# A two-layer relational graph convolution: each ring buffer of ten gathered row tiles is filled and read in the opposite direction on every other pass

## The chip, the cores and the metric

The kernel runs on one core of a Trainium2 chip. The metric is the device time of one execution in microseconds (us), as the median of three runs; lower is better.

## The reference

There are N = 50000 nodes with D = 128 numbers each, 850000 edges sorted by their destination, 16 relations and 8 basis matrices. Two layers of a relational graph convolution are followed by a residual sum and a layer norm. Everything is in 32-bit floats.

```python
def _rgcn_layer(h, src, dst, rel, basis, w_comp, loop_w, bias):
    W = jnp.einsum('rb,bio->rio', w_comp, basis)            # 16 x 128 x 128
    seg = dst * 16 + rel
    agg = jax.ops.segment_sum(h[src], seg, num_segments=50000 * 16)
    agg = agg.reshape(50000, 16, -1)
    msg = jnp.einsum('nri,rio->no', agg, W)
    return jax.nn.relu(msg + h @ loop_w + bias)

h = _rgcn_layer(x, src, dst, rel, basis1, w_comp1, loop_w1, bias1)
h = _rgcn_layer(h, src, dst, rel, basis2, w_comp2, loop_w2, bias2)
return _layernorm(x + h)
```

The heavy part is `h[src]`: for every edge, a row of 128 floats (512 B) has to be fetched from a place in memory that an index gives.

## The kernel before, in words

**Tiles and chunks.** 128 edges make a tile. K = 10 tiles make a chunk, and a layer has C = 625 chunks (800000 edges; each node's edge to itself is treated apart, without a gather). The layers are the rounds n = 0 and n = 1 of one loop: layer 0 reads its rows from `x`, layer 1 from `H1`, the DRAM tensor that layer 0 wrote. In all there are 1250 chunks and 12500 tiles.

**Gathers.** One gather fetches the 128 rows of one tile by an indirect DMA of the Pool engine (`gather`, L198). Every gather of the program has this line, because the line is the helper's. It writes slot k of a row buffer. There are GATHERS = 6 row buffers of ten slots each, used in turn as a ring: chunk c of layer n has buffer `(n * C + c) % GATHERS`.

```python
for to in range(0 if c == 0 else c + FETCH, min(C, c + FETCH + 1)):
    for k in range(ks(to)):
        gather(rows[(n * C + to) % GATHERS][:, k, :], of, src[:, to * K + k : to * K + k + 1])
```

`ks(to)` is the number of tiles of a chunk (ten). FETCH = 2 fixes only the place of the gathers in the program's text. The engines run apart from each other, each through its own instructions in order, so Pool runs ahead until it would overwrite a slot that TensorE has not read yet.

**What a chunk does.** For each tile, TensorE multiplies the gathered rows (as the stationary operand) with `hot`, a 128 x 96 matrix that VectorE makes (`hot_of`, L782 and L789) and that says which of the tile's up to 12 destinations an edge belongs to, weighted for the 8 bases (L837, tile `pa`). Five tiles (PER = 5, half a chunk) share one PSUM bank; after them ScalarE copies the bank to `aT` (L844). So a chunk has two halves, each with five gathers' rows, five multiplications and one copy. Each fp32 multiplication shows as two TensorE records in the profile.

**What lies between.** Between the two halves of chunk c, `slots` multiplies `aT` of chunk c - 1 with the eight bases, all accumulating in `ps` (L689), and ScalarE copies the result (L693). Ahead of the first half, `nodes_of` adds up the slots of chunk c - 2 by node (L703, L707, tile `pn`; VectorE's sum L709; ScalarE's `kept`, L712) and stores the nodes' result. The nodes' own parts (`from_itself`, 391 tiles of 128 nodes per layer) are spread over the chunks, at most chunks one and at some none: a transpose (L205), its copy `hT` (L207), the product with the bases `hb` (L667), which VectorE weighs (L670) and reduces (L681), and a store (L682). In layer 0 a preparation of later rows (`coming`) runs between the chunks too; Pool takes part in it with twenty scatters.

**Who sets the order.** TensorE's and Pool's instructions run in the order in which the program writes them (a manual schedule for these two engines). The waits between the engines are put in by the framework from what reads and writes which tile: an instruction that overwrites a slot waits for the semaphore of the engine that read it, unless its engine has already waited for that point or a later one. Ahead of an instruction that needs a second wait stands a semaphore instruction of its own.

Of the kernel before, what the change touches and what calls it, by code (L numbers as in the profile page):

```python
# [64 lines left out]
PER = 5  # L65
Q = AT // 2
GATHERS = 6
# [9 lines left out]
def tile_rgcn_resnorm(  # L77
# [20 lines left out]
    C = -(-M // (K * P))  # L98
# [98 lines left out]
    def gather(to, of, idx):  # L197
        nc.gpsimd.indirect_dma_start(  # L198
            out=to, out_offset=None, in_=of, in_offset=bass.IndirectOffsetOnAxis(ap=idx, axis=0)
        )  # L200
# [382 lines left out]
    def chunked():  # L583
        with (
# [5 lines left out]
            def at(c):  # L590
                return nc.values_load(
                    base_i[0:1, c : c + 1],
                    engines=[mybir.EngineType.SP],
                    min_val=0,
                    max_val=N - P,
                    skip_runtime_bounds_check_because="bases are clamped to N - P, and no node is below 0",
                )

            def weights(c, n):

                m = min(AT, 2 * (C - c)) * NR
                rel = hp.tile([P, LIVE], U8, name="rel")
                nc.sync.dma_start(
                    rel[:m],
                    bass.AP(
                        tensor=REL.tensor, offset=REL.offset + 2 * c * LIVE, ap=[[LIVE, m // NR], [0, NR], [1, LIVE]]
                    ),
                )
                is_rel = hp.tile([P, LIVE], F32, name="is_rel")
                nc.vector.tensor_scalar(is_rel[:m], rel[:m], its_rel[:m], None, op0=OP.is_equal)  # L610
                yield
                pm = ps_m.tile([P, AT * PER * NB], F32, name="pm")
                of = pm.rearrange("e (t j) -> e t j", t=AT)
                for j in range(PER):
                    nc.tensor.matmul(  # L615
                        of[:, :, j * NB : (j + 1) * NB],
                        is_rel[:m, j * P : (j + 1) * P],
                        EACH[n][:m],
                        start=True,
                        stop=True,  # L620
                    )
                yield pm.rearrange("e (t b) -> e t b", b=NB)
# [104 lines left out]
            def asked(c):  # L727

                return min(NT, -(-(c + 1) * NT // C) + AHEAD)
# [40 lines left out]
            for n, of in enumerate((x, H1)):  # L770

                kept, summed_up, multiplied, lws = None, None, None, []
                base, ks = [at(0), None, None], lambda c: min(K, -(-M // P) - c * K)
                own_parts = []

                def own_nodes(c):

                    return range(asked(c - 1) if c > 1 else 0, asked(c) if c else 0)

                def hot_of(c, pm):  # L780
                    own = hp.tile([P, K, WN], F32, name="own")
                    nc.vector.tensor_tensor(  # L782
                        own[:, : ks(c)],
                        grid[:, None, :WN].to_broadcast([P, ks(c), WN]),
                        key[:, c * K : c * K + ks(c), None].to_broadcast([P, ks(c), WN]),
                        op=OP.is_equal,
                    )
                    hot = hp.tile([P, K, NB, WN], F32, name="hot")
                    nc.vector.tensor_tensor(  # L789
                        hot[:, : ks(c)],  # L790
                        pm[:, c % Q * K : c % Q * K + ks(c), :, None].to_broadcast([P, ks(c), NB, WN]),
                        own[:, : ks(c), None, :].to_broadcast([P, ks(c), NB, WN]),
                        op=OP.mult,
                    )
                    return hot

                def loaded(n0):

                    ls = sb.tile([P, D], F32, name="ls_of")
                    nc.sync.dma_start(ls, L[n][ds(n0, P), :])  # L800
                    xw = None
                    if n:
                        xw = sb.tile([P, D], F32, name="xw")
                        nc.sync.dma_start(xw, x[ds(n0, P), :])
                    return ls, xw

                weigh = weights(0, n)
                next(weigh)
                for c in range(C):
                    now[0] = c  # L810
                    if n == 0 and c:

                        next(coming, None)
                        while ready[0] + 1 < len(ROWS) and 2 * min(C, c + FETCH + 4) > ROWS[ready[0] + 1]:
                            next(coming)
                    if c:
                        base = [at(c)] + base[:2]
                    for to in range(0 if c == 0 else c + FETCH, min(C, c + FETCH + 1)):
                        for k in range(ks(to)):
                            gather(rows[(n * C + to) % GATHERS][:, k, :], of, src[:, to * K + k : to * K + k + 1])  # L820
                    g = rows[(n * C + c) % GATHERS]
                    if c == 0:
                        if n == 0:
                            done(first_runs)
                        pm = next(weigh)
                        hot = hot_of(c, pm)
                    if c > 1:
                        kept = nodes_of(kept, c - 2, ks(c - 2), summed_up, base[2], *others, n)
                        others = loaded(base[1])
                    parts = own_parts[0] if own_parts else iter(())  # L830
                    next(parts, None)
                    aT = hp.tile([P, NB, S], F32, name="aT")
                    for k in range(0, ks(c), PER):
                        m = min(PER, ks(c) - k)
                        pa = ps_a.tile([P, BANK], F32, name="pa")
                        for i in range(m):
                            nc.tensor.matmul(  # L837
                                pa[:, i * NB * WN : (i + 1) * NB * WN],
                                g[:, k + i, :],
                                hot[:, k + i].rearrange("e b w -> e (b w)"),  # L840
                                start=True,
                                stop=True,
                            )
                        nc.scalar.copy(  # L844
                            aT[:, :, k * WN : (k + m) * WN].rearrange("d b (i w) -> d i b w", w=WN),
                            pa[:, : m * NB * WN].rearrange("d (i b w) -> d i b w", i=m, w=WN),
                        )
                        if k == 0:
                            next(parts, None)
                            if c:  # L850
                                summed_up = slots(c - 1, ks(c - 1), multiplied, n)
                            next(parts, None)
                    multiplied = aT
                    for parts in own_parts:
                        done(parts)
                    if c == 1:
                        others = loaded(base[1])
                    if c + 1 < C:
                        if (c + 1) % Q == 0:
                            pm = next(weigh)  # L860
                        hot = hot_of(c + 1, pm)
                        if c + 2 < C and (c + 2) % Q == 0:
                            weigh = weights(c + 2, n)
                            next(weigh)
                        own_parts = []
                        for i in own_nodes(c + 1):
                            own_parts.append(from_itself(i, of, n, lws))
                            if len(own_parts) == 1:
                                next(own_parts[0])
                    if n == 0 and c == 3:  # L870
                        beginning.close()
                    if n == 0 and c == C - 1:
                        done(coming)
                        count_up(pr)
                last = loaded(base[0])
                kept = nodes_of(kept, C - 2, ks(C - 2), summed_up, base[1], *others, n)
                summed_up = slots(C - 1, ks(C - 1), multiplied, n)
                nodes_of(kept, C - 1, ks(C - 1), summed_up, base[0], *last, n)
# [189 lines left out]
```

## Time and profile before

| what | value |
|---|---|
| median of three runs | 18938.22 us (18929.84 to 18953.83) |
| the profiled execution | 18936.72 us |
| its span, from first to last instruction | 18934.8 us |
| granted TensorE clock, mean | 0.72 of full speed |
| TensorE matmuls (PE) | 10703.0 us, 57% of the span, 59198 records |
| TensorE weight loads (PEld, overlap PE) | 9174.1 us, 48% |
| VectorE (DVE) | 6595.5 us, 35% |
| ScalarE (ACT) | 2775.4 us, 15% |
| Pool (POOL) | 11864.7 us, 63%, 12533 instructions |
| DMA queue of the gathers (q0) | 403552 packets, 826.82 MB, 16.8% of 16 engines' time |
| all transfers | 1227.02 MB, mean 65 GB/s |

How to read the lines of this profile. A group of instructions is named by its line (L198 is line 198 of the kernel), engine, operation, and tiles: `g<-H,src` writes a row buffer `g` from `H` by the indices in `src`. Behind `x` is the count, behind the first bar the busy time in us and the mean of one in ns, behind the second bar the idle time of the engine just ahead of such instructions and what ended it. A row of the waits has the waiting engine, tile and line, then what let it go, then the sum of these waits in us, their number, and the longest of them. "issue" is time in which the engine waited for nothing that the profile shows. "remote" means that a semaphore let the instruction go, but no instruction or transfer that the profile shows ended near that moment. A row of the timeline has the start in us from the span's start, the duration, the engine, the line, what was done, and in brackets the idle time ahead of it with its releaser.

### The profile page before, as it was taken

What the parts mean: (1) busy time and instruction counts of PE and PEld (TensorE: products, weight loads), DVE (VectorE), ACT (ScalarE), POOL (GpSimd) and SP (SyncE); (2) the same over time, 40 slices, a digit from 0 to 9 for tenths busy, and PEclk for the clock granted to TensorE, in tenths of its full rate; (3) what the DMA queues carried; (4) which work ended last, traced back from release to release, by engine and by line L of the source; (5) the groups of instructions that cost most, each with busy time, mean ns of one, the idle gap of its engine ahead of it and who ended that gap; (6) DMA issues with size and microseconds to landing.
All of it is one profiled execution on the core that took longest, in us unless ns stands there. A gap on an engine that the chain in (4) does not pass through costs nothing.

```text
span 18934.8 us, 187693 instructions
## 1 busy us (share of the span) xinstructions
PE 10703.0 (57%) x59198; PEld 9174.1 (48%) x59198; DVE 6595.5 (35%) x14269; ACT 2775.4 (15%) x7815; POOL 11864.7 (63%) x12533
## 2 busy tenths in 40 slices
PE   4555555555555555555555555555555555555555
PEld 3444445444544445445445555445454444444445
DVE  4333334333333332333223333333333333333333
ACT  1111111111111111111111111111111111111111
POOL 5666666665666666666656666666666666666665
PEclk7777777676777776777767777777777777777777
DMA  2222222222222222222222222222222222222222
GB/s 80 69 69 65 68 66 66 66 66 63 62 62 61 61 61 61 61 61 61 61 55 66 67 66 67 66 66 67 65 66 66 66 66 66 65 66 66 66 65 62
DMA packets 1164943, 1227.02 MB, mean 65 GB/s; under 512 B 283055, under 2 KB 952401, under 8 KB 1163937
## 3 DMA queue, kind: packets, MB, share of 16 engines
q0 software_dynamic: 403552, 826.82, 16.8%
q1 hardware_dynamic: 757169, 386.65, 7.1%
q8 instruction: 472, 7.73, 0.2%
q14 instruction: 534, 4.37, 0.1%
q10 hardware_dynamic: 3216, 1.45, 0.0%
HBM read 1059.55 MB, written 154.23 MB: 64 GB/s over the span
## 4 chain that ended last, share of the span: by engine, by line
another core or an unknown queue 22%; PE 17%; issue 7%; DVE 5%; ACT 2%; DMA 0%; POOL 0%; SPq 0%; ACTq 0%; DVEq 0%; POOLq 0%
PE pa L837 6%; PE ps L689 4%; PE hb L667 4%; DVE ls L681 1%; DVE by L670 1%; DVE hot L789 1%; PE pn L703 1%; ACT aT L844 1%; PE pn L707 1%; PE po L678 0%; PE po L205 0%; DVE by L679 0%; ACT slots L693 0%; ACT sd L574 0%
## 5 line engine op out<-in xcount | busy, mean ns | idle before, releaser
L198 POOL DMA_INDIRECT g<-H,src x6250 | 5910.6, 946 | 3393.7 <-issue 1422.2
L198 POOL DMA_INDIRECT g<-in_x_dram,src x6250 | 5927.4, 948 | 3338.4 <-issue 1411.5
L837 PE MATMUL pa<-hot,g 128*128 128x96 f32 x25000 | 4125.3, 326 | 1898.8 <-DVE hot L789 1388.2
L837 PEld LDWEIGHTS pa<-hot,g 128*128 128x128 f32 x25000 | 4014.2, 243 | 2402.1 <-DVE hot L789 1434.6
L689 PEld LDWEIGHTS ps<-basis,aT 128*120 128x120 f32 x20000 | 3222.4, 240 | 927.1 <-issue 849.3
L667 PE MATMUL hb<-basis,hT 128*128 128x512 f32 x3128 | 2273.3, 818 | 2107.1 <-ACT hT L207 915.7
L689 PE MATMUL ps<-basis,aT 128*120 128x128 f32 x20000 | 3211.3, 329 | 224.3 <-issue 150.5
L670 DVE TENSOR_TENSOR by<-hb,lw 128x512 f32<-128x512 f32 x1564 | 1080.1, 691 | 6152.1 <-remote 2557.6
L789 DVE TENSOR_TENSOR hot<-pm,own 128x960 f32<-128x960 f32 x1250 | 1432.6, 1153 | 4113.1 <-remote 3585.2
L844 ACT COPY aT<-pa 128x480 f32<-128x480 f32 x2500 | 1395.2, 558 | 6619.3 <-remote 3577.7
L703 PE MATMUL pn<-slots,own 120*128 120x128 f32 x2500 | 708.5, 373 | 2448.5 <-ACT slots L693 1502.1
L703 PEld LDWEIGHTS pn<-slots,own 120*128 120x128 f32 x2500 | 470.3, 235 | 2593.2 <-ACT slots L693 1583.3
L667 PEld LDWEIGHTS hb<-basis,hT 128*128 128x128 f32 x3128 | 638.1, 253 | 2191.4 <-ACT hT L207 943.1
L681 DVE TENSOR_REDUCE ls<-by 128x128 f32<-128x1152 f32 (+1 forms) x782 | 1656.9, 2119 | 12.1
L693 ACT COPY slots<-ps 120x128 f32<-120x128 f32 x1250 | 332.4, 266 | 5771.4 <-remote 3733.1
L205 PE MATMUL po<-ident,h_own 128*128 128x128 f32 (+1 forms) x782 | 295.8, 378 | 1151.9 <-issue 399.5
L205 PEld LDWEIGHTS po<-ident,h_own 128*128 128x128 f32 (+1 forms) x782 | 138.1, 177 | 1219.9 <-issue 415.1
L707 PE MATMUL pn<-kept,shift 128*128 128x128 f32 x2496 | 604.8, 332 | 12.1 <-DVE shift L706 6.3
L615 PE MATMUL pm<-each,is_rel 128*128 128x64 f32 x3140 | 438.6, 281 | 114.4 <-issue 110.4
L707 PEld LDWEIGHTS pn<-kept,shift 128*128 128x128 f32 x2496 | 493.7, 245 | 14.2 <-DVE shift L706 7.7
L712 ACT COPY kept<-pn 128x128 f32<-128x128 f32 x1248 | 336.1, 269 | 1079.7 <-DVE a L709 603.5
L709 DVE TENSOR_TENSOR a<-pn,ls_of 128x128 f32<-128x128 f32 x1250 | 355.1, 284 | 386.6 <-remote 133.1
(148 smaller groups left out, 5082.0 us busy)
## 6 DMA issues: line engine op xcount, KB each, us to landing
g<-in_x_dram,src POOLq DMA_INDIRECT x6250
g<-H,src POOLq DMA_INDIRECT x6250
ls_of<-L SPq DMA_DIRECT2D x1250, 64.0 KB
L<-ls SPq DMA_DIRECT2D x780, 64.0 KB
H<-h SPq DMA_DIRECT2D x625, 64.0 KB
xw<-in_x_dram SPq DMA_DIRECT2D x625, 64.0 KB
out_dram<-o SPq DMA_DIRECT2D x625, 64.0 KB
h_own<-in_x_dram SPq DMA_DIRECT2D x390, 64.0 KB
```

What stands on the lines that cost most here:

```text
L198: nc.gpsimd.indirect_dma_start(out=to, out_offset=None, in_=of, in_offset=bass.IndirectOffsetOnAxis(ap=idx, axis=0))
L205: nc.tensor.transpose(tp[:, :m], h, ident[:m, :m])
L615: nc.tensor.matmul(of[:, :, j * NB : (j + 1) * NB], is_rel[:m, j * P : (j + 1) * P], EACH[n][:m], start=True, stop=True,)
L667: nc.tensor.matmul(hb[:m], hT, BASIS[n][:, b : b + few, :].rearrange("p b d -> p (b d)"), start=True, stop=True)
L670: nc.vector.tensor_tensor(by[:m, b : b + few, :], hb[:m].rearrange("p (b d) -> p b d", d=D), lw[:m, b : b + few, None].to_broadcast([m, fe ...
L681: nc.vector.tensor_reduce(ls[:m], by[:m].rearrange("p b d -> p d b"), AX.X, OP.add)
L689: nc.tensor.matmul(ps[: k * WN], aT[:, b, : k * WN], BASIS[n][:, b, :], start=b == 0, stop=b == NB - 1)
L703: nc.tensor.matmul(pn, own[: k * WN], st[: k * WN], start=True, stop=not c)
L707: nc.tensor.matmul(pn, shift, kept, start=False, stop=True)
L789: nc.vector.tensor_tensor(hot[:, : ks(c)], pm[:, c % Q * K : c % Q * K + ks(c), :, None].to_broadcast([P, ks(c), NB, WN]), own[:, : ks(c), ...
L837: nc.tensor.matmul(pa[:, i * NB * WN : (i + 1) * NB * WN], g[:, k + i, :], hot[:, k + i].rearrange("e b w -> e (b w)"), start=True, stop=True,
L844: nc.scalar.copy(aT[:, :, k * WN : (k + m) * WN].rearrange("d b (i w) -> d i b w", w=WN), pa[:, : m * NB * WN].rearrange("d (i b w) -> d i ...
```

## The change

Chunks are counted over both layers, `n * C + c`, and the count divided by six (the number of buffers) gives the pass over the ring. On an even pass nothing differs from before. On an odd pass the ten gathers of a chunk fill the slots from 9 down to 0, and the ten multiplications read them in that order: the second half first, and within each half the last tile first. The `slots` step and the own-node steps stay between the half that is read first and the one that is read second. No instruction of another kind is added, and none of the gathers, multiplications or copies is removed. `base`, `hot_of`, the ring of buffers, FETCH and the order of the chunks are untouched.

```diff
+                def in_turn(c, k, of=None):
+
+                    of = of or range(k)
+                    return list(of)[:: 1 - 2 * ((n * C + c) // GATHERS % 2)]
+
...
                     for to in range(0 if c == 0 else c + FETCH, min(C, c + FETCH + 1)):
-                        for k in range(ks(to)):
+                        for k in in_turn(to, ks(to)):
                             gather(rows[(n * C + to) % GATHERS][:, k, :], of, src[:, to * K + k : to * K + k + 1])
...
-                    for k in range(0, ks(c), PER):
+                    halves = list(range(0, ks(c), PER))
+                    for k in in_turn(c, len(halves), halves):
                         m = min(PER, ks(c) - k)
                         pa = ps_a.tile([P, BANK], F32, name="pa")
-                        for i in range(m):
+                        for i in in_turn(c, m):
                             nc.tensor.matmul(
...
-                        if k == 0:
+                        if len(halves) == 1 or k == halves[in_turn(c, len(halves))[0]]:
                             next(parts, None)
                             if c:
                                 summed_up = slots(c - 1, ks(c - 1), multiplied, n)
```

A buffer is thus refilled in the reverse of the order in which it was last read: the slot that was read last is written first.

## The prediction

> **What bounds the kernel now.** I read the page from the top: busy time, groups, the chain, then the waits, then stretches of the timeline. No engine is full:
>
> ```profile
> PE 10703.0 (57%) x59198; PEld 9174.1 (48%) x59198; DVE 6595.5 (35%) x14269; ACT 2775.4 (15%) x7815; POOL 11864.7 (63%) x12533
> another core or an unknown queue 22%; PE 17%; issue 7%; DVE 5%; ACT 2%; DMA 0%; POOL 0%; SPq 0%; ACTq 0%; DVEq 0%; POOLq 0%
> L198 POOL DMA_INDIRECT g<-H,src x6250 | 5910.6, 946 | 3393.7 <-issue 1422.2
> L198 POOL DMA_INDIRECT g<-in_x_dram,src x6250 | 5927.4, 948 | 3338.4 <-issue 1411.5
> ```
>
> A gather is 0.95 us busy and 0.30 us of "issue", a pitch of 1.25 us, and POOL does nothing else of weight: 12500 x 1.25 = 15625 us of the 18934.8. The rest is stops. The largest share of the chain belongs to no engine, so I ask the waits who waits there:
>
> ```profile
> ACT slots L693 <- remote: 3733.1, 551, 49.8
> DVE hot L789 <- remote: 3585.2, 428, 24.9
> ACT aT L844 <- remote: 3577.7, 570, 35.9
> POOL g L198 <- PE pa L837: 1621.8, 1277, 33.9
> POOL g L198 <- remote: 1586.1, 1153, 8.9
> ```
>
> Every "remote" row of size waits on TensorE's own semaphore, at a time when no matmul ended by the profile in the 1.5 us before. So a matmul's completion is seen late. A table of stretches shows when (after the stretch: PE, PEld, DVE, ACT, POOL busy with counts, granted clock, DMA share, GB/s):
>
> ```profile
> 9593.00:9618.00 25.00, 24.39 (x202) 24.04 (x200) 10.02 (x26) 8.54 (x24) 0.00 (x0) 0.93 0.11 31
> 9645.00:9715.00 70.00, 10.89 (x36) 8.07 (x36) 0.69 (x1) 0.83 (x2) 52.94 (x57) 0.52 0.20 53
> ```
>
> In the first, POOL is silent (all gathers of layer 0 are issued): PE is full and a chunk takes 4.42 us. In the second POOL gathers without a pause into buffers that are long free, and everything else stands still. The timeline inside it:
>
> ```profile
> 9648.38 3.35 PE L689 MATMUL ps<-basis,aT 128*120 128x128 f32 x16
> 9662.53 0.56 ACT L844 COPY aT<-pa 128x480 f32<-128x480 f32 x1 [20.14 <-remote]
> 9668.08 0.69 DVE L670 TENSOR_TENSOR by<-hb,lw 128x512 f32<-128x512 f32 x1 [25.33 <-remote]
> 9712.87 0.27 ACT L693 COPY slots<-ps 120x128 f32<-120x128 f32 x1 [49.79 <-remote]
> ```
>
> The `ps` matmuls end at 9651.7 by the profile; ScalarE is let go for them at 9712.87. So back-to-back gathers hold back what the other engines may see of each other. In the steady part this makes a cycle: POOL gathers until the ring of six buffers is full, stops, completions come through, POOL goes on.
>
> ```profile
> 9050.44 0.94 POOL L198 DMA_INDIRECT g<-in_x_dram,src  x1 [0.30 <-issue]
> 9053.60 0.94 POOL L198 DMA_INDIRECT g<-in_x_dram,src  x1 [2.22 <-remote]
> 9054.84 0.94 POOL L198 DMA_INDIRECT g<-in_x_dram,src  x1 [0.30 <-issue]
> ```
>
> Counted over all gathers of the trace (a stop: next start over 1.5 us later; gather n is slot n mod 10 of its chunk): 1473 stops, 3190 us. 447 stand before slot 0 (1538 us, median 2.8), 734 before slot 5 (1359 us, median 2.0), 292 elsewhere. Updates of TensorE's semaphore recorded per us: 1.2 in a run's first two gathers, 0.3 from the fourth on, 0.1 from the twentieth; 0.4 in the first half us of a stop, 1.6 in the next, 7.2 between 1.5 and 2.0 us. So each stop first costs some 1.5 us of nothing, and each restart gives about 3 us of free progress. The mean chunk, from chunk 60 to 1200, takes 15.04 us; 1250 x 15.04 = 18800 leaves 137 us for start and end of the profiled execution's 18936.7, which is 1.5 us under the median of the three runs, 18938.2. So: time = 137 + 1250 x cycle.
>
> **The change, part by part.** *Order of reading and of filling.* The same 25000 matmul records, 2500 copies and 12500 gathers, in another order; within a chunk a matmul still reads the slot that was gathered at the same place of the order. Nothing by itself. POOL's two scatters of the preparation (20 in all) keep their places between chunks.
>
> *Waits that go.* Now each gather waits for TensorE's reading of its own slot six chunks ago, and has one semaphore instruction before it (12506 on POOL). After it, the first gather of a chunk writes the slot that was read last; when it may go, so may the other nine, which should lose their wait on TensorE and most of their semaphore instructions. Price of these: 4316 gathers with none between them and the gather before start after 0.305 us (median), 3057 with two also after 0.305. They hide behind the gather ahead. If that cover were gone, the recorded 0.017 us x some 11000 = 190 us. I take zero.
>
> *The wait that is added.* The first gather now waits for the tenth matmul and not for the first; queued behind it are nine gathers. Those who need their rows are the matmuls of six chunks later: from a gather's end to its matmul the trace has 82.7 us (median, first slot; 78.4 the last; 5% under 71). The delay is at most from first half to last: 8.6 us between the two `aT` copies of a chunk. The rows stay early.
>
> *The stops.* What remains is the rhythm: POOL no longer starts when half a chunk is free, and no longer stops at slot 5; it gathers ten without a pause, then stops until the last matmul of the next chunk is seen. The trace has that very situation, shifted by five slots: a run that starts at slot 5 (second half just seen) and goes on for ten. From 687 such starts to the copy of the next chunk's second half:
> - 367 runs (53%) go exactly ten gathers: 15.0 us. Kept.
> - 117 (17%) go 11 to 14 and then take 18.1, having begun a second burst on single slots. After the change they stop at ten: I take 15.0.
> - 112 (16%) go 15 or more: the half was seen in time. They become runs of twenty. Now, after fifteen, POOL stops 3.5 us for the first half of the next chunk, and the second half is seen 7.3 us later. Twenty gathers take 25 us; the stop behind them lies between 5.0 (then the pair takes 30, as now) and 10.8 (3.5 + 7.3). Nearer the low end, as TensorE has had six more us: 6.5, the pair 31.5.
> - 91 (13%) stop before ten, since TensorE is late. That stop now comes after the tenth, after more starving: between 15.0 and 12.5 + 6.1 = 18.6; I take 16.0.
>
> Per 99 starts: 70 x 15.0 + 16 x 31.5 + 13 x 16.0 = 1762 us for 115 chunks, 15.32 us. 137 + 1250 x 15.32 = **19290 us**, 1.9% slower. With the low ends 15.0 (18890), with the high ones (doubles 35.8, late 18.6) 16.2 (20390).
>
> Two rules weighed. The row: PE's clock is 0.52 in the starved stretch and 0.93 in the free one. The Trainium skill (TensorE: Matmul & The Clock Gate, HAM oscillation) says that pauses over some 3.4 us put TensorE back to half clock; longer unbroken bursts make more such pauses, which speaks against the change; if every matmul ran at half clock, PE's 10703 us at 0.72 would be 15400, 12.3 us a chunk. And where the rows show completions held back by gathers, the skill (DMA: Bandwidth & Descriptors, Anatomy of one DMA) calls a DMA's semaphore write almost free on trn2; by that nothing would be held back and POOL alone would set 12.5 us a chunk before and after, which the 70 us stretch contradicts.
>
> **Rivals.** *One stop a chunk pays (faster).* There are 1.18 stops a chunk now, 2.16 us each. If every cycle locks into the exact run of ten with the 2.0 us stop that follows it in the trace (372 cases, quartiles 1.98 to 2.09), the cycle is 14.5: 18290; with some late halves 14.9: 18760. For it: 74% of the runs before a chunk that has an own-node part go exactly ten. Against: before chunks without one only a third do. It decides if stops of over 4 us stay under one in ten.
>
> *Relief (faster).* If POOL's waits on TensorE's semaphore are what holds it back, they go, and POOL is bound at 12.5 us: about 15800. Against: the first 60 gathers (44 to 121 us) wait on no matmul, and TensorE's updates come 5.6 us apart there too.
>
> *Nothing happens.* The framework keeps ten per chunk, or the cycle stays by chance at 15.0: 18940.
>
> **How the numbers follow.** Slower as worked out: 0.58 (own range 18980 to 20390). One stop pays: 0.30. Relief: 0.04. Nothing: 0.08, which is all within 0.2%, about what a measurement of this kernel can tell from no change. Faster is 0.30 + 0.04 = 0.34. The range leaves out relief, the lowest part of the locked case, and the slow tail: 18450 to 20200.
>
> **What would show it.** Right: runs of gathers only in multiples of ten, all stops before the first gather of a chunk, gather pitch still 1.25 us, "remote" still the largest waits, some stops of 5 us and more behind runs of twenty. Wrong: stops nearly all at 2.0 us (locked), or almost no stops and full TensorE clock (relief). A pitch under 1.25 us would make the semaphore instructions a cost after all.

## The result: 3.8% slower, and the profile after

The changed kernel takes 19651.8 us (median of four runs, 19629.3 to 19667.7) where the kernel before takes 18934.0: a ratio of 1.0378, 95% interval 1.0360 to 1.0396. The forecast said slower, by 1.9% (19290); the time lies inside the range, but the loss is 718 us where 352 were forecast, twice as much. The profiled execution took 19629.3 us, its span is 19627.5, the granted clock 0.716 (before 0.720).

The page of the changed kernel: busy time, the chain, and the two groups of gathers.

```profile
PE 10992.7 (56%) x59198; PEld 9425.0 (48%) x59198; DVE 6594.1 (34%) x14269; ACT 2779.3 (14%) x7815; POOL 11894.5 (61%) x12533
another core or an unknown queue 21%; PE 17%; issue 8%; DVE 5%; ACT 1%; POOL 0%; DMA 0%; DVEq 0%; ACTq 0%; SPq 0%; POOLq 0%
L198 POOL DMA_INDIRECT g<-H,src x6250 | 5933.2, 949 | 3793.8 <-issue 1732.5
L198 POOL DMA_INDIRECT g<-in_x_dram,src x6250 | 5934.5, 950 | 3633.5 <-issue 1739.9
```

The number of gathers is the same and their price nearly so (946 and 948 ns before, 949 and 950 now). The idle time ahead of gathers grew from 6732.1 to 7427.3 us, by 695.2: as much as the two spans differ, 692.7. The "issue" part of it hardly matters: between gathers that follow each other the mean pitch is 1.2526 us before and 1.2521 after. So the time went into stops. The waits of the changed kernel (lines have moved by up to six: L850 is the `aT` copy, L794 `hot`, L843 `pa`):

```profile
ACT aT L850 <- remote: 5097.1, 725, 28.9
DVE by L670 <- remote: 4226.5, 347, 49.7
DVE hot L794 <- remote: 3514.0, 480, 53.7
POOL g L198 <- remote: 1390.9, 591, 11.1
POOL g L198 <- PE pa L843: 1374.5, 211, 27.6
POOL g L198 <- PE po L678: 988.8, 121, 16.4
```

"remote", the completions that are seen late, still lead. Pool's waits for TensorE are fewer and longer: 923 in these three rows, 4.1 us in the mean, where the two rows of before have 2430 of 1.3 us. In the third row it is a product of an own-node part (`po`) that ends the wait. Counted over all gathers: 1050 stops and 3889 us, before 1473 and 3196. 956 of the 1050 stand ahead of the first gather of a chunk; none of weight is left at the sixth (7 stops, 3 us). The lengths of the runs of gathers between stops, chunks 60 to 1200: 578 of ten, 213 of twenty, four or fewer of any longer multiple; 43 tens are cut into six and four by a gap of 0.3 us. From stop to stop at a chunk's start, ten take 14.84 us (639 cases) and twenty take 33.36 (229 cases): 16.7 a chunk. The mean cycle is 15.60 us; before it was 15.04. So the twenties are the whole loss: chunks that all took 14.84 us would be faster than before (an estimate, from these two numbers).

A run of twenty in Pool's timeline, with the stop behind it and the run of ten that follows:

```profile
8627.70 0.95 POOL L198 DMA_INDIRECT g<-in_x_dram,src  x1 [2.23 <-remote]
...
8651.47 0.94 POOL L198 DMA_INDIRECT g<-in_x_dram,src  x1 [0.30 <-issue]
8661.16 0.94 POOL L198 DMA_INDIRECT g<-in_x_dram,src  x1 [8.74 <-PE pa L843]
...
8672.42 0.95 POOL L198 DMA_INDIRECT g<-in_x_dram,src  x1 [0.30 <-issue]
8675.60 0.95 POOL L198 DMA_INDIRECT g<-in_x_dram,src  x1 [2.23 <-remote]
```

Twenty gathers, a stop of 8.74 us; ten gathers, a stop of 2.23. What the other engines did meanwhile, by stretches (first ten, second ten, the long stop, the ten after it; columns as in the table of stretches above):

```profile
8627.70:8640.20 12.50, 6.45 (x41) 6.22 (x41) 2.86 (x4) 2.09 (x6) 9.46 (x10) 0.80 0.26 68
8640.20:8652.70 12.50, 6.20 (x28) 4.96 (x28) 2.50 (x5) 0.27 (x1) 9.46 (x10) 0.77 0.23 58
8652.70:8661.10 8.40, 4.37 (x14) 3.33 (x15) 2.98 (x8) 1.26 (x5) 0.00 (x0) 0.50 0.09 25
8661.10:8675.60 14.50, 9.29 (x63) 7.68 (x61) 5.77 (x10) 2.09 (x7) 9.46 (x11) 0.85 0.25 64
```

In the second ten ScalarE does one instruction of 0.27 us: the engines hardly see each other's work any more. Why the stop is so long shows in their own timeline:

```profile
8655.99 0.69 DVE L670 TENSOR_TENSOR by<-hb,lw 128x512 f32<-128x512 f32 x1 [13.29 <-remote]
8656.00 0.56 ACT L850 COPY aT<-pa 128x480 f32<-128x480 f32 x1 [13.80 <-remote]
8656.73 2.08 PE L667 MATMUL hb<-basis,hT 128*128 128x512 f32 x2 [9.55 <-DVE by L670]
8658.60 2.29 PE L843 MATMUL pa<-hot,g 128*128 128x96 f32 x10
```

VectorE and ScalarE, idle for 13 us, are let go 3.6 us after the run's last gather has ended (8652.41). The half of the chunk that Pool waits for still has everything ahead of it: a product with the bases, which needs VectorE's `by`, and then its own ten records. Only at 8661.16 can Pool go on.

### The profile page after: what moved, and what is told of

It is laid out like the page before. It is cut to its first block, busy times and chain, and to the rows that moved or that the text cites. A ratio compares the mean times of both kernels' runs of the same rounds, so it can differ in the third digit from the quotient of the medians.

```text
span 19627.5 us, 176498 instructions
## 1 busy us (share of the span) xinstructions
PE 10992.7 (56%) x59198; PEld 9425.0 (48%) x59198; DVE 6594.1 (34%) x14269; ACT 2779.3 (14%) x7815; POOL 11894.5 (61%) x12533
## 3 DMA queue, kind: packets, MB, share of 16 engines
q0 software_dynamic: 403552, 826.82, 16.7%
q10 hardware_dynamic: 3216, 1.45, 0.0%
## 4 chain that ended last, share of the span: by engine, by line
another core or an unknown queue 21%; PE 17%; issue 8%; DVE 5%; ACT 1%; POOL 0%; DMA 0%; DVEq 0%; ACTq 0%; SPq 0%; POOLq 0%
PE pa L843 6%; PE hb L667 4%; PE ps L689 4%; DVE ls L681 1%; DVE by L670 1%; DVE hot L794 1%; PE pn L703 1%; PE pn L707 1%; PE po L678 1%; PE pm L615 1%; DVE by L679 0%; PE po L205 0%; ACT aT L850 0%; DVE own L699 0%
## 5 line engine op out<-in xcount | busy, mean ns | idle before, releaser
L843 PEld LDWEIGHTS pa<-hot,g 128*128 128x128 f32 x25000 | 4169.2, 251 | 2477.9 <-issue 1261.5
L843 PE MATMUL pa<-hot,g 128*128 128x96 f32 x25000 | 4255.1, 333 | 1919.9 <-DVE hot L794 1121.0
L667 PE MATMUL hb<-basis,hT 128*128 128x512 f32 x3128 | 2372.6, 851 | 3097.6 <-DVE by L670 2065.7
L689 PEld LDWEIGHTS ps<-basis,aT 128*120 128x120 f32 x20000 | 3295.3, 246 | 1148.6 <-issue 1122.8
L689 PE MATMUL ps<-basis,aT 128*120 128x128 f32 x20000 | 3306.4, 336 | 450.2 <-issue 425.2
L794 DVE TENSOR_TENSOR hot<-pm,own 128x960 f32<-128x960 f32 x1250 | 1432.1, 1152 | 3876.1 <-remote 3514.0
L850 ACT COPY aT<-pa 128x480 f32<-128x480 f32 x2500 | 1384.9, 559 | 7931.9 <-remote 5097.1
L679 DVE TENSOR_TENSOR by<-po,bias 128x128 f32<-128x128 f32 (+1 forms) x782 | 223.7, 286 | 968.8 <-remote 678.5
L207 ACT COPY hT<-po 128x128 f32<-128x128 f32 (+1 forms) x782 | 208.5, 267 | 2061.7 <-remote 1093.9
```

The source lines that it names most:

```text
L667: nc.tensor.matmul(hb[:m], hT, BASIS[n][:, b : b + few, :].rearrange("p b d -> p (b d)"), start=True, stop=True)
L689: nc.tensor.matmul(ps[: k * WN], aT[:, b, : k * WN], BASIS[n][:, b, :], start=b == 0, stop=b == NB - 1)
L794: nc.vector.tensor_tensor(hot[:, : ks(c)], pm[:, c % Q * K : c % Q * K + ks(c), :, None].to_broadcast([P, ks(c), NB, WN]), own[:, : ks(c), ...
L843: nc.tensor.matmul(pa[:, i * NB * WN : (i + 1) * NB * WN], g[:, k + i, :], hot[:, k + i].rearrange("e b w -> e (b w)"), start=True, stop=True,
L850: nc.scalar.copy(aT[:, :, k * WN : (k + m) * WN].rearrange("d b (i w) -> d i b w", w=WN), pa[:, : m * NB * WN].rearrange("d (i b w) -> d i ...
```

## The experiments

Seventeen runs were made. They were taken in seven groups, and each is compared with the kernel before on the same chip in the same group. That turned out to matter more than anything else.

### The same kernels where nothing is held back

The first four runs were meant to take the change apart. The edits:

```diff
# e1_fill_back: kernel before, filled backwards on every pass, read forwards
-                        for k in range(ks(to)):
+                        for k in reversed(range(ks(to))):
# e2_both_back: changed kernel, filled and read backwards on every pass
-                    return list(of)[:: 1 - 2 * ((n * C + c) // GATHERS % 2)]
+                    return list(of)[::-1]
# e3_by_half: changed kernel, only the five tiles inside a half in turn
-                        for k in in_turn(to, ks(to)):
+                        for k in [h + i for h in range(0, ks(to), PER) for i in in_turn(to, min(PER, ks(to) - h))]:
-                    for k in in_turn(c, len(halves), halves):
+                    for k in halves:
...
-                        if len(halves) == 1 or k == halves[in_turn(c, len(halves))[0]]:
+                        if k == 0:
# e4_every_own: changed kernel, an own-node part in every chunk
                 def own_nodes(c):
+                    if c > 1 and asked(c - 1) == asked(c):
+                        return range(asked(c) - 1, asked(c))
```

> Every chunk is filled from slot 9 down to 0 and read from 0 up, on every pass; nothing alternates, and the matmuls keep the order of before. Theory A (what costs is that a chunk is released as a whole: the first gather waits for the last matmul, so gathers run in tens and twenties): as the changed kernel, 19550 to 19750 us, nearly all stops ahead of the first gather of a chunk, about one run in four a run of 20, with a stop of over 8 us behind it. Rival B (what costs is reading in turn forwards and backwards): as before, 18900 to 19000 us. Rival C (the last-gathered row is now read first, so rows come late): above 19750 us.

> Every chunk is filled and read from slot 9 down to 0, on every pass: slots come free in the order in which they are filled, as before, but the second half is always read first. Theory A: 18850 to 19000 us, stops mainly at the first and the sixth gather of a chunk. Rival B (the reversed order itself costs, half of the passes having cost 3.8%): 19650 to 20400 us.

> The first half always comes before the second, in filling and in reading; only the five tiles inside each half are taken forwards and backwards in turn. So gathers are released in fives. Theory A: no stop but at the first and the sixth gather, the 292 stops elsewhere (236 us in all) are gone, runs of 5, 10 and 15, no or few runs of 20: 18650 to 18950 us. Rival D (the loss grows evenly with the number of gathers that one wait releases: 1 at 18938, 10 at 19652): 4/9 of the loss, about 19250 us.

> The changed kernel with more work: each of the chunks without an own-node part does the last such part once more (some 460 more transposes, products and stores of values that are already there). Theory A: a run of 20 starts only where the next chunk has no own-node part (201 of 410 such starts, against 11 of 466 with one), and 20 cost 33.4 us where two runs of 10 cost 29.7. With a part in every chunk the runs of 20 go, and in spite of the added work the time falls: 137 + 1250 x 14.9 = 18760, range 18600 to 19000 us. Rival E (the other engines' work sets the time): some 460 times a few us more, 20500 us or more.

None of these expectations was met, nor could be. The kernel before took 15825 us in this group. The four took 15817, 15823, 15823 and 15850 (ratios 0.9995, 1.0000, 0.9998, each within 0.001, and 1.0016). Busy time, the chain and the gathers on the page of e3_by_half:

```profile
PE 11794.8 (75%) x59198; PEld 9629.8 (61%) x59198; DVE 6574.0 (42%) x14269; ACT 2781.2 (18%) x7815; POOL 11899.6 (75%) x12533
POOL 34%; issue 18%; PE 15%; DMA 11%; DVE 1%; ACT 0%; POOLq 0%; SPq 0%; DVEq 0%; ACTq 0%
L198 POOL DMA_INDIRECT g<-in_x_dram,src x6250 | 5943.6, 951 | 1935.3 <-issue 1746.3
L198 POOL DMA_INDIRECT g<-H,src x6250 | 5930.1, 949 | 1939.5 <-issue 1739.1
```

And the two longest of its waits:

```profile
ACT aT L850 <- PE pa L843: 7403.8, 2435, 47.1
DVE by L670 <- PE hb L667: 5104.5, 1475, 16.4
```

A gather costs the same (950 ns and 0.30 of issue), but "remote" is gone from the chain and the head of the waits; each engine sees the other's work when it ends. Pool gathers almost without a stop (94 stops, 109 us in all), and a chunk takes 12.5 us in layer 1. That is the time of the prediction's rival "Relief" to within 0.4% (137 + 1250 x 12.5 = 15762, against 15825), brought about not by the change but by the conditions of the run.

Two conditions are thus found, and all kernels of one group meet the same one: the kernel before took 15807 to 15825 us in three groups, and 18921 to 19061 in the four others and 18934 beside the changed kernel. The traces differ in one more thing. A gather raises its semaphore in 16 steps; 12500 x 16 = 200000. The trace of e3_by_half holds 199580 such steps one by one, that of the kernel before 41295: where completions are held back they also arrive in lumps. The traces of all runs sort in this way, about 200000 in nine of them and 39000 to 62000 in the others. What sets the condition no run here shows. It is not the chip alone: the record has chip 4 both for e13 to e15, where nothing was held back, and for e16 and e17, eleven minutes later, where completions were.

### The change in both conditions, and a pause

```diff
# e6_pause (10), e10_pause7 (7), e12/e14/e17_pause5 (5): changed kernel, ahead of each chunk's gathers
+    idle_t = consts.tile([P, 64], F32, name="idle_t")
...
+                        for _ in range(10):
+                            nc.gpsimd.iota(
+                                idle_t, pattern=[[1, 64]], base=0, channel_multiplier=0, allow_small_or_imprecise_dtypes=True
+                            )
```

> The changed kernel itself, once more beside the kernel before. In the four runs ahead of this one the kernel before took 15825 us and not 18934, with no wait for a completion that is seen late: Pool gathered without a stop. Theory A (the change costs time only where back-to-back gathers hold completions back): if the kernel before takes about 15825 here, the changed one does too, within 0.2%; if it takes about 18930, the changed one takes 19650. Rival B (reading in turn costs by itself): above the kernel before by 3 to 4% in both cases.

> The changed kernel with a pause of Pool of about 2 us ahead of each chunk's ten gathers: ten small iota instructions into a tile that nothing reads. Theory A: each pause lets the completions through that ten gathers held back, and no run of 20 can form, so where completions are held back the cycle is 12.5 + 2.0 to 2.5 = 14.5 to 15.0 us, 18260 to 18890 us, faster than the changed kernel by 4 to 7% in spite of 2500 to 3000 us of added work on the busiest engine. Where they are not held back, the same cycle and so the same 18260 to 18890 us, now 15 to 19% slower than without the pause. Rival F (only a stop of Pool's gathers that waits on a semaphore lets them through, or Pool's own instructions hold them back too): where completions are held back, slower than the changed kernel by about the pauses, 21000 us or more.

Here completions were held back. The changed kernel repeated its loss: 19800.7 against 19060.7, ratio 1.0383 (1.0366 to 1.0400). With the pause it took 19216 us, 3.0% less, although Pool has 12500 instructions more to do. The added instruction in the groups of e6_pause:

```profile
L826 POOL IOTA idle_t<- 128x64 f32 x12500 | 2341.3, 187 | 779.1
```

And its first waits:

```profile
ACT aT L855 <- PE pa L848: 7179.6, 1564, 24.4
ACT slots L694 <- PE pa L848: 4252.0, 978, 6.8
DVE by L671 <- PE hb L668: 3685.9, 661, 20.9
```

"remote" is gone from the head of the list: a pause is enough for completions to come through, and it need not be a wait. So rival F falls. The time lies above the expected 18890 since the pause was longer than intended: ten times 0.25 us and 0.2 around them make 2.71 (the median of the stops ahead of a chunk; 5% to 95%: 2.70 to 2.92). With their mean, 137 + 1250 x (12.5 + 2.76) = 19212 is nearly the measured time: ahead of almost every chunk the pause is the whole stop. The rows now come only 1.7 us (median) before their matmuls, so it is Pool that sets the pace.

### Where the runs of twenty come from

Pool starts on ten gathers when TensorE has read a chunk; the next chunk that TensorE reads is the one whose end lets Pool's second ten go. Sorted by what that next chunk holds, the changed kernel's trace gives a rule: of the starts whose next chunk has no own-node part 201 of 410 become a run of twenty, of those whose next chunk has one, 11 of 466. It fits that a light chunk is finished and seen while Pool still gathers the first ten, so that Pool goes straight into the second. If that is the cause, adding work to the light chunks must make the kernel faster.

> The changed kernel with the last own-node part done once more in each chunk that has none, as in the run e4_every_own, where nothing was held back and it took 15850 us. Where completions are held back (kernel before at 18900 to 19100): theory A, a run of 20 starts only where the next chunk has no own-node part, so with a part in every chunk the runs of 20 go and the time falls below the changed kernel's in spite of the added work: 137 + 1250 x 14.9 = 18760, range 18600 to 19100 us. Rival E (the other engines' work sets the time): above the changed kernel by 460 times a few us, 20500 us or more. Where nothing is held back: 15850 us again.

Beside the kernel before at 19061 us the changed kernel's level is 1.0383 x 19061 = 19791. e7_every_own took 18956 us: ratio to the kernel before 0.9939 (0.9922 to 0.9956). 476 own-node parts more, and the whole loss is gone and a little more. Runs of ten 1051, of twenty 3; ten gathers and their stop take 15.00 us. Where nothing is held back the same work cost 24 us in 15825 (e4_every_own). One other thing moved: the granted clock was 0.736, and 0.711 in e5_after_again. It can have only a small part: in the trace of e5_after_again a twenty takes 3.75 us more than two tens, and its 194 twenties are thus 730 us of the 835 that e7_every_own is under the changed kernel's level (an estimate, across two groups).

The opposite way, cutting the twenties with a pause only there:

```diff
# e8_pause_light: changed kernel
+                        q = n * C + to - GATHERS
+                        if q >= 0 and not len(own_nodes(q % C)):
+                            for _ in range(8):
+                                nc.gpsimd.iota(
+                                    idle_t,
...
```

> The changed kernel with a pause of Pool of about 2.2 us (eight small iota instructions) only ahead of those chunks (38 in 100) whose slots were last read by a chunk without an own-node part: the places where a second ten could follow the first without a stop. Theory A: every run of 20 is cut in two; two tens with a pause of 2.2 and a stop of 2.3 take 29.5 us where a run of 20 with its stop took 33.5 (213 runs in the steady part), so 18700 to 18950 us where completions are held back, 3.5 to 5% under the changed kernel. Rival G (the loss lies in the later release of all chunks, not in the runs of 20): no faster than the changed kernel, 19600 to 20300 us, since pauses are added. Where nothing is held back: 15825 + 478 x 2.2 = 16900 us at most.

19172 us, ratio 1.0059 (1.0039 to 1.0079): most of the loss is gone, but less than expected. At the paused places no run of twenty is left (0 of 370 starts). But 128 runs of twenty are there now, 90 of them at starts (283) where two chunks with a part follow each other; in the changed kernel those had 9 of 147. The pause may give the chunk behind it a head start, so that it is seen early in its turn; no run tested that. "A light chunk" is then not the whole rule; a chunk that is seen before the tenth gather would be. Rival G falls: added pauses took away 619 of the 730 us.

### Release or order; length of the pause

> As e1_fill_back: filled from slot 9 down on every pass, read from 0 up on every pass. Where completions are held back (kernel before at 18900 to 19100): theory A (release of a chunk as a whole, with light chunks giving runs of 20), 3.3 to 4.3% slower than the kernel before, stops only ahead of a chunk's first gather, runs of 20 about one in four. Rival B (reading in turn costs by itself): within 0.5% of the kernel before.

> As e6_pause with seven iota instructions in place of ten ahead of each chunk: a pause of 1.95 us (e6: 2.71 for ten, so 0.25 each and 0.2 around them). Where completions are held back, theory A: completions come through 1.5 to 2.0 us into a stop, so 1.95 us are just enough to keep the other engines in step with Pool; cycle 12.5 + 1.95 = 14.45, 137 + 1250 x 14.45 = 18200 us, at most 18500, under the kernel before. Rival H (the rows were only 1.7 us early in e6, so the other engines were at their own limit of 15.3 us a chunk there): 19100 us or more, and stops return. Where nothing is held back: 18000 to 18300 us.

e9_fill_back, which reads forwards in every chunk, took 19763 us against 18921: ratio 1.0445 (1.0428 to 1.0463), a little above the expected band, with 231 runs of twenty among 574 of ten. Reading in turn is not needed for the loss; what this kernel shares with the changed one is the release of a chunk as a whole, on every pass. Rival B falls. The kernel that fills and reads backwards on every pass (e2_both_back) was not run where completions are held back.

e10_pause7 took 18302 us: ratio 0.9675 (0.9659 to 0.9692). It beats both kernels, and rival H falls. All but 43 of the 1249 stops ahead of a chunk are the pause itself (median 1.95 us), the cycle is 14.58 us, and the rows still lie ready 15 us ahead (median, first slot). Its longest "remote" wait of `aT` is 10.2 us where the changed kernel's is 28.9:

```profile
ACT aT L855 <- PE pa L848: 3621.8, 1087, 26.6
ACT aT L855 <- remote: 2328.1, 529, 10.2
```

Two kernels remained, the release in fives and a shorter pause. Twice they met the condition in which nothing is held back, with a ring of four buffers (`GATHERS = 4`) beside them the second time:

> As e3_by_half: the first half always ahead of the second, the five tiles of each half forwards and backwards in turn, so gathers are released in fives. Where completions are held back (kernel before at 18900 to 19100): theory A, no stop but ahead of the first and the sixth gather, the ragged stops are gone, few runs of 20, so level with the kernel before or under it by up to 1.5%. Rival D (the loss grows evenly with the number of gathers that one wait releases): slower than the kernel before by 4/9 of 3.8 to 4.4%, 1.7 to 2.0%.

> As e10_pause7 with five iota instructions: a pause of 1.45 us ahead of each chunk. Where completions are held back, theory A: TensorE's updates come at 0.4 per us or less until 1.5 us into a stop and at 8 per us from 1.5 to 2.0, so a pause of 1.45 us ends just before they come through; Pool stops for TensorE again, with longer stops, and the time is above that of e10_pause7 although less work is added: 18500 to 19800 us. Rival I (any pause helps in proportion, the other engines keep pace): 137 + 1250 x 13.95 = 17570 us, at most 17900.

> The kernel of e11_by_half, for a chip that holds completions back (kernel before at 18900 to 19100). Theory A: no stop but ahead of the first and the sixth gather of a chunk, few runs of 20, level with the kernel before or under it by up to 1.5%. Rival D (the loss grows evenly with the number of gathers that one wait releases): 1.7 to 2.0% slower. Where nothing is held back: 15805 us again.

> The kernel of e12_pause5, for a chip that holds completions back. Where nothing was held back it took 17678 us, so its pauses are 1872 / 1250 = 1.50 us each. Theory A: completions come 1.5 to 2.0 us into a stop, so the pause ends just before them, Pool stops for TensorE again, and the time is above the 18302 us of the pause of 1.95 us although less is added: 18500 to 19800 us. Rival I (the other engines keep pace): 17680 us, as where nothing is held back.

> The changed kernel with a ring of four row buffers in place of six. Theory A: the rows lie ready some 75 us ahead of their matmuls with six buffers, and two chunks less leave over 40; the rhythm of tens and twenties is the same, so within 1.5% of the changed kernel's 19650 to 19800 us where completions are held back. Rival C (the later release hurts because a slot is refilled too late): with two buffers less slower than the changed kernel by 3% or more, with lead times of the rows near zero. Where nothing is held back: 15800 to 15900 us.

e11 and e13 took 15807 and 15806 us (ratio 0.9999 both times), e15_ring4 15802 (0.9997). e12 and e14 took 17678 and 17677 against 15807: there the five iotas are a plain cost of 1870 us, 1.50 per chunk. The ring of four was not run where completions are held back; that the shorter distance plays no part there rests on the trace alone, in which rows wait 76.9 us (median, first slot) for their matmul. Then, in the other condition:

> The kernel of e11 and e13 once more, both of which met no holding back. Where completions are held back (kernel before at 18900 to 19100): theory A, stops only ahead of the first and the sixth gather, few runs of 20, level with the kernel before or under it by up to 1.5%; rival D (the loss grows evenly with the number of gathers that one wait releases), 1.7 to 2.0% slower.

> The kernel of e12 and e14 once more. Where completions are held back: theory A, the pause of 1.50 us ends before they come through, Pool stops for TensorE again, 18500 to 19800 us; rival I (the other engines keep pace), 17680 us, as where nothing is held back.

e16_by_half took 18690 us against 18935: ratio 0.9864 (0.9847 to 0.9880), a little *faster* than the kernel before. Runs of ten 574, fifteen 265, five 103, and two of twenty. Stops other than at the first and sixth gather fell from 292 to 72 (from 298 us, not the 236 that the first expectation gave, to 45). Releasing five at once costs nothing, ten costs 3.8%: rival D falls, the loss does not grow evenly with the number released but comes with the twenties.

e17_pause5 took 18604 us, ratio 0.9823 (0.9807 to 0.9840). It does less added work than e10_pause7 and is 302 us slower; where nothing is held back it took 17677. Of its stops ahead of a chunk a quarter are the bare pause (1.45 us) but the median is 2.01 and the upper quartile 2.30: for most chunks 1.5 us end before the completions come through. Rival I falls, as in the changed kernel's own trace: TensorE's updates come at 0.4 per us in the first us of a stop and at 8.4 between 1.5 and 2.0 us.

## Why the prediction was right in sign and half in size

**The bound and the mechanism** were right: gathers hold completions back, time is 137 us plus 1250 cycles. The changed kernel has 1250 x 15.60 + 137 = 19637 us. (Two numbers of the prediction are slightly off, without effect: the stops of before add up to 3196 us and not 3190, and a locked cycle of 14.5 us gives 18262 and not 18290.)

**Waits that go** were rightly put at nothing. 11195 instructions fewer are in the trace (187693 to 176498), and the pitch moved by 0.0005 us.

**The wait that is added** did not starve TensorE of rows: their lead is 76.9 us at the first slot and 74.6 at the last.

**The stops.** Shape right: tens and twenties, all stops of weight at the chunk's start. Three sizes were off. In steady cycles of ten and twenty:

| term, put right one after the other | forecast | measured | the cycle then (from 15.32 us) |
|---|---|---|---|
| a ten with its stop (70 at 15.0, 13 at 16.0) | 15.16 us | 14.84 us | 15.09 us |
| a twenty with its stop | 31.5 us | 33.36 us | 15.35 us |
| share of twenties among the starts | 16 of 99 | 229 of 868 | 15.61 us |

The last is (639 x 14.84 + 229 x 33.36) / 1097; 137 + 1250 x 15.61 = 19650. The errors in the tens and in the twenties' price cancel, by luck; what is left of the miss is the share.

**The step that failed**, the third of these, is the sorting of the 117 runs of 11 to 14 gathers: "After the change they stop at ten: I take 15.0." They had gone past ten, so the next chunk's reading was already coming through. The share of twenties rose from the forecast 16 of 100 starts to 26, which is what about six in ten of these 117 would add (an estimate; no trace can follow one start into the other kernel). The trace of before pointed there: among starts whose next chunk has no own-node part, 93 of 346 went 11 to 14 and 93 went 15 or more, together 54%; after the change 49% of such starts are twenties. The prediction used the split by own-node parts only as evidence for a rival, and not to sort the cases.

The price of a twenty was off by its stop, put at 6.5 us "as TensorE has had six more us". It is 8.5 us (mean). The stretch above shows one such case, in which the other engines did next to nothing in the second ten.

**The rivals.** "One stop pays" named the right ideal: e7_every_own and e10_pause7, whose runs are nearly all tens, go at 15.0 and 14.58 us. The condition it gave, stops of over 4 us in under one of ten, is what the change fails: 28% of its stops ahead of a chunk are longer, against 4% in e7_every_own. "Relief" was ruled out rightly for the condition of the first profile; its time, though not its cause, is what the other condition gives. "Nothing happens" holds there, for every order of filling and reading tried (the changed kernel itself was run there only with four buffers, e15_ring4, and with added work, e4_every_own).

**The two rules weighed.** The mean clock hardly moved (0.720 to 0.716), so TensorE was not held at half clock throughout. But the stretch of the long stop above has 0.50, and over all stops behind a run of twenty the clock is 0.60, behind a run of ten 0.71. How much of the 8.5 us this costs no run separates; the `pa` records inside these stops take 365 ns and 355 (means), which points to little. The Trainium skill (DMA: Bandwidth & Descriptors, Anatomy of one DMA) counts the semaphore update among the small parts of a DMA, some 100 ns after its data are confirmed; the condition without holding back agrees with the 12.5 us a chunk that the prediction drew from it (15825 us); in the other, with engines let go 13 us late, more than that is at work, and what comes late there is also TensorE's own semaphore, of which that passage does not speak.

## What to carry to other kernels

When two engines hand a ring to and fro and the producer disturbs the rest, merging many small waits into one large one changes the rhythm, not just the number of waits: ask when the producer will run through the place where it used to stop. Sort such cases by what the consumer has to do next, since the light steps are the ones that let the producer run away. And run the kernel before beside every experiment: here its own time moved by a sixth between groups of runs, and in one of the two conditions every order tried was worth the same. Release in fives is the version to keep of those tried, 1.4% faster in the one condition and level in the other; the pause of 1.95 us gains 3.3% in the one, and a pause of 1.50 us already cost 11.8% in the other.

## What the runs showed of the hardware that was not expected

The holding back is no fixed trait of these instructions: with the same gathers at the same pitch of 1.25 us it was there in the profiles of before and after and in four later groups of runs, and absent in three, and with it goes whether the 200000 semaphore steps of the gathers show singly or as 39000 to 62000. Where it is there, a stop of the gathers has to last about 2 us to let completions through, whether it is a wait or a row of small iotas of 187 ns: a pause of 1.50 us was too short ahead of most chunks, one of 1.95 us was enough for Pool ("remote" waits stay, up to 10.2 us for `aT`), and with 2.71 us they are gone from the head of the waits. In the changed kernel the last gather of a run has raised its semaphore 2.28 us (median) after its start, and TensorE's first completions come through about 2.9 us after it, so it looks as if they queue behind the gathers' own; no run tested that queue.
